# One order for an attention turn, base products issued ahead of the expert weights, loads and stores spread over more queues

## The chip, the cores and the metric

The kernel runs on one core of one Trainium2 chip. The metric is the device time of one execution in microseconds (us); smaller is better. The time before is the median of three runs.

Five engines work side by side, each through its own queue of instructions in order: PE (matrix products, with PEld its weight loads), DVE (vector work, the only one used here for maxima), ACT (scalar functions and copies), POOL (general vector work) and SP (which only issues DMAs). ACT and POOL can issue DMAs too. Matrix products land in eight PSUM banks of 128 x 512 float32.

## The reference, cut to what matters

The input is 2 sequences of 1024 tokens with 512 features. Three blocks follow one another, each on a layer norm (LN) of its input, added to it:

```
x = x + 0.5 * ffn(layernorm(x))
x = x + attn(layernorm(x))
x = x + 0.5 * ffn(layernorm(x))      # the same weights again

ffn(x):   base = x @ W_base.T + b_base                    # 512 x 512
          w    = the 2 largest of softmax(x @ W_router.T), renormalised, 8 experts
          h    = x @ lora_A[e].T  (rank 16, 8 experts = 128 columns)
          base + 2 * sum_e w[e] * (h[e] @ lora_B[e].T)
attn(x):  q, k, v = x @ sign(W).T * scale, cleaned of NaN and infinities
          32 query heads, 8 key/value heads, head size 16
          softmax(q k.T / 4) v, then the output projection of the same kind
```

## The kernel before, in words

**Groups.** Tokens are worked on in groups of 512 (`GT`), written (batch, group): (0,0), (0,1), (1,0), (1,1). A group is four tiles of 128 tokens. `first` does the first FFN, the second LN and q, k, v of a group; `second`, `rest`, `last` and `final` do the output projection and the last FFN. q, k and the attention's output go through DRAM (`qd`, `kd`, `ad`) to be laid out by head.

**An FFN (`ffn_tiles`, line 346).** LN and transposes give `xT`. The router and the rank-16 products come as one matmul of 136 columns (`low`, tile `ph`). Then a chain of small DVE steps picks two experts (lines 385 to 419), the weighted hidden values are transposed and copied to `hT` (line 432), and only then the strands `base(t)` (line 436) are started. Each first adds the bias to the residual on POOL (line 439), does four accumulating matmuls with `wb` (line 444, each two float32 passes), a fifth with `lb` on `hT` (line 448), and adds the result to the residual (line 451 on DVE in the head and the tail, lines 456 and 459 on ACT and POOL during the attention). In the traces, the tiles of the first FFN have names that end in `f`, those of the last FFN names that end in `s`; `hT` is needed by line 448 alone.

**A planner writes the order out.** Each piece of work is a Python generator ("strand") that yields the engine that it needs next: `P` (PE), `v` (DVE), `a` (ACT), `g` (POOL), `d` (SP). `Flow.offer(kind)` gives one step to the first strand by rank whose due time has come; due times and costs are in planner ticks of 0.115 us (`usec`). All of it happens when the program is built: what comes out is a fixed order for each engine. `flow.free` is true in the head (before the attention) and in the tail (after it). `flow.stock` counts what may be held at once, `fb` being PSUM banks: 6 in the head and the tail, 2 for strands during the attention. The pool of banks has 7 and the attention's sums have the eighth.

**The attention (line 868).** There are 32 units (batch, half of the queries, key/value head), each of 4 query heads. A unit takes four turns. A turn does, for three units at different stages: 8 `m` tiles (scores with queries on the partitions, line 785, for the row maxima on DVE, line 793); 8 `e` tiles (transposed scores in two accumulating matmuls, `e0` line 820 and `e1` line 824, the second of which subtracts the maximum, then the exponential on ACT, line 827); and 32 small products with v, `A0` to `A3`, 8 passes each (line 857). An `m` or `e` matmul uses half of the PE's rows, the upper or the lower by the parity of its index, so that two neighbours of different parity run side by side. `A` and the strands' matmuls use all rows. Each `m` and each `e` tile takes a PSUM bank until DVE or ACT has read it.

The order within a turn is written out by hand. Letters are places at which a strand may get a step: `F` for PE, `V` and `W` for DVE, `C` and `D` for ACT; POOL and SP are offered a step after every item. `S` places the maxima of a unit. There are two orders. `FULL` has two `F` (one at either end) and a planned length of 64 ticks, and is taken where PE work of a strand waits; `BARE` has none and 50 ticks:

```
order = (LEAD_IN if not e and not a else FULL if flow.wants("P", begin + at_F)
         else BARE)
span = BRIEF if order is BARE else TICK
```

`need` holds the turns back where q, k or v of a unit are not yet there, and hands out strands' steps until they are.

**The head.** SP issues in this order: the four tiles of x(0,0), `arw` (expert and router weights), `wb` (1 MB), x(0,1), `lb`, then the attention's weights (line 87) with x(1,0) between them. POOL issues the bias `bh` and the scales, then does memsets, among them `two_r` and `mqs` (lines 112 to 117). DVE scales `bh` by one half (line 105). `begin` (line 745) does half of the first unit's `m` tiles when k and the first q of (0,0) are stored, and loads the second half of its keys (`place_k`, line 742) when k of (0,1) is stored. `qkv_part` (line 524) makes each q, k and v item: a scaled copy `y`, cleaning into `o`, then the high part in `y` by ACT (line 568) and the rest in `o` by POOL or DVE (line 571); SP stores both with two DMAs each (line 577).

Of the kernel before, what the change touches and what calls it, by code (L numbers as in the profile page):

```python
# [8 lines left out]
F32 = mybir.dt.float32  # L9
# [6 lines left out]
P = 128  # L16
# [16 lines left out]
def macaron_kernel(ctx: ExitStack, tc: tile.TileContext, x_in, wbT, b_base, wrT, aT, bT,  # L33
# [25 lines left out]
    def load_x(b, g):  # L59
        t = xpool.tile([P, TG, D], F32, tag="x", name=f"x{b}_{g}")  # L60
        for i in range(TG):
            nc.sync.dma_start(t[:, i, :], x_in[b, g * GT + i * P:g * GT + (i + 1) * P, :])
        xg[b, g] = t
# [6 lines left out]
    nc.sync.dma_start(wb, wbT.rearrange("(c p) n -> p c n", p=P))  # L70
# [34 lines left out]
    nc.vector.tensor_scalar(bh, bh, 0.5, None, ALU.mult)  # L105
# [6 lines left out]
    nc.gpsimd.memset(two_r.bitcast(F32), 0.0)  # L112
    for h in range(REP):
        nc.gpsimd.memset(two_r.bitcast(F32)[32 * h:32 * h + 2, h % 2, :], 1.0)
    mqs = [const.tile([P, 512], F32R, name=f"mq{i}") for i in range(3)]
    for t in mqs:
        nc.gpsimd.memset(t.bitcast(F32), 0.0)
# [6 lines left out]
    TICK, BRIEF = 64, 50  # L124
# [15 lines left out]
    class Flow:  # L140
# [79 lines left out]

        def wants(self, kind, by):
            self.settle()
            return any(s.kind == kind and s.at <= by and (kind != "P" or self.lock in (None, s))
                       for s in self.strands)
# [121 lines left out]
    def ffn_tiles(xt, name, rank, tiles, xT, hT, mv, given, mv2, summed, store, loads):  # L346
# [35 lines left out]
        yield "j", list(s2.values())  # L382

# [50 lines left out]
        ready = flow.t  # L434

        def base(t):
            yield "r", dict(t=1)
            yield "g", ""
            nc.gpsimd.tensor_tensor(xt[:, t, :], xt[:, t, :], bh, ALU.add)  # L439
            for c in range(KC):  # L440
                yield ("P", "P") if c else ("P", "", flow.t, 1)
                if c == 0:
                    pb = bank(f"pb{n}_{t}")
                nc.tensor.matmul(pb, xT[:, c, t * P:(t + 1) * P], wb[:, c, :],  # L444
                                 start=(c == 0), stop=False)
                flow.lock = bs[t] if c < KC - 1 else None
            yield "P", "a", ready
            nc.tensor.matmul(pb, hT[0][:, t * P:(t + 1) * P], lb, start=False, stop=True)  # L448
            if flow.free:
                yield "v", "P"  # L450
                nc.vector.scalar_tensor_tensor(xt[:, t, :], pb, 0.5, xt[:, t, :], ALU.mult, ALU.add)
                flow.give(t=1, fb=1)
            else:
                yield "a", "P"
                hb = t512(f"hb{n}_{t}")
                nc.scalar.activation(hb, pb, AF.Copy, scale=0.5)  # L456
                flow.give(fb=1)
                yield "g", "a"
                nc.gpsimd.tensor_tensor(xt[:, t, :], xt[:, t, :], hb, ALU.add)  # L459
                flow.give(t=1)  # L460
            if store is not None:
                yield ("a" if flow.free else "d"), "v" if flow.free else "g"
                (nc.scalar if flow.free else nc.sync).dma_start(store[t * P:(t + 1) * P, :],
                                                                xt[:, t, :])
            if mv2 is not None:
                yield "v", "v" if flow.free else "g"
                stats(xt, t, mv2, n)
                summed.add(t)

        bs = {}  # L470
        for t in tiles:
            bs[t] = flow.spawn(base(t), rank)
# [51 lines left out]
    def qkv_part(b, g, xs, i, fast, at):  # L524
# [40 lines left out]
        if i <= KC:  # L565
            yield "a", "v"
            hi = y[:, :].bitcast(F32R)
            nc.scalar.copy(hi, o)  # L568
# [146 lines left out]
    def places(order, span):  # L715
        w = [LOAD.get(o[0], 0) for o in order]
        return [span * sum(w[:i]) // sum(w) for i in range(len(w))]
# [352 lines left out]
```

## Time and profile before

| | us |
|---|---|
| median of 3 runs | 1160.85 (1159.07 to 1164.19) |
| the profiled execution | 1162.21 |
| its span, first to last instruction | 1160.2 |
| PE, DVE, ACT, POOL busy in the span | 1068.2, 878.5, 669.8, 287.6 |
| mean granted PE clock | 0.968 of full |

The head lasts from 0 to about 162 us (the first products with v start there), the attention to about 1089 us, the tail to the end. "Busy" counts an engine's instructions, and PE's are pipelined: a busy PE is not a PE at its peak. In the windows view each engine's busy time in a stretch is followed by its number of instructions, and the last three columns are the granted PE clock, the busy share of the 16 DMA engines and GB/s.

### The profile page before, as it was taken

The numbers are of one execution on the slowest core, as the hardware profiler recorded it, in microseconds if no ns is written. First come the engines' busy times: TensorE is split into PE (matmuls) and PEld (weight loads), VectorE is DVE, ScalarE is ACT, GpSimd is POOL, SyncE is SP. The second block draws the span as 40 slices with busy tenths as digits, with TensorE's granted clock in tenths as the row PEclk, the third lists the DMA queues.
The fourth block names the chain that finished last, engine by engine and source line by source line (L and its number), as shares of the span: only waits on it lengthen the run. The fifth ranks groups of instructions, "written<-read, shape, count | busy, mean of one in ns | idle before, by whom it ended". The sixth has DMA issues, their size and how long they took to land.

```text
span 1160.2 us, 21527 instructions
## 1 busy us (share of the span) xinstructions
PE 1068.2 (92%) x8453; PEld 589.0 (51%) x8453; DVE 878.5 (76%) x1694; ACT 669.8 (58%) x1309; POOL 287.6 (25%) x337
## 2 busy tenths in 40 slices
PE   3989679999999999999989899999999999999988
PEld 2446435554455554455555455644445555444544
DVE  5577978787788787778788898698779878874372
ACT  2222238765667566667746568665667766666611
POOL 4142632000110031112163322032011213421161
PEclk9989759999999999999989999999999999999989
DMA  8012453121111123214334342112222411221101
GB/s 272 3 61 77 140 174 105 47 47 47 47 47 47 47 83 118 48 40 106 106 87 144 83 114 57 47 47 56 56 65 64 120 45 36 67 84 47 55 24 50
DMA packets 48686, 87.43 MB, mean 75 GB/s; under 512 B 8760, under 2 KB 11832, under 8 KB 48584
## 3 DMA queue, kind: packets, MB, share of 16 engines
q1 hardware_dynamic: 47176, 83.36, 24.9%
q10 hardware_dynamic: 1152, 2.10, 0.5%
q8 instruction: 66, 1.08, 0.4%
q0 software_dynamic: 256, 0.59, 0.3%
q14 instruction: 36, 0.29, 0.1%
HBM read 51.19 MB, written 34.32 MB: 74 GB/s over the span
## 4 chain that ended last, share of the span: by engine, by line
PE 71%; DVE 18%; DMA 3%; ACT 3%; POOL 2%; issue 2%; SPq 0%; POOLq 0%; DVEq 0%; ACTq 0%
PE av L857 19%; PE m L785 15%; DVE mn L793 9%; PE e L820 9%; PE e L824 7%; PE pbf L444 5%; PE pbs L444 4%; PE po L668 2%; ACT es L827 2%; DMA x<-in_x 2%; PE pq L538 2%; PE pv L555 1%; PE pbf L448 1%; PE pbs L448 1%; PE phs L368 1%
## 5 line engine op out<-in xcount | busy, mean ns | idle before, releaser
L793 DVE TENSOR_REDUCE mn<-m 128x1 f32<-128x512 f32 x1024 | 647.6, 681 | 161.5 <-PE e L824 86.0
L827 ACT ACTIVATE es<-e 128x512 f32<-128x512 f32 x1024 | 542.4, 602 | 305.9 <-PE e L824 254.0
L785 PE MATMUL m<-k 64*128 64x512 f32 x1024 | 365.1, 443 | 27.6 <-DMA k<-kd 12.9
L857 PE MATMUL av<-es,vaug 128*32 128x256 f32 x4096 | 277.7, 389 | 18.9 <-ACT es L827 9.3
L820 PE MATMUL e<-k 64*128 64x512 f32 x1024 | 277.8, 443 | 2.7 <-DVE mn L793 2.5
L785 PEld LDWEIGHTS m<-k 64*128 64x128 f32 x1024 | 169.4, 188 | 175.9 <-DVE mn L793 77.8
L824 PE MATMUL e<-mq,two_r 64*128 64x512 f32 x1024 | 255.7, 399 | 1.9 <-DMA mq<-mT 1.9
L857 PEld LDWEIGHTS av<-es,vaug 128*32 128x32 f32 x4096 | 108.6, 110 | 148.8 <-issue 83.9
L820 PEld LDWEIGHTS e<-k 64*128 64x128 f32 x1024 | 121.8, 187 | 61.2 <-DVE mn L793 33.0
L824 PEld LDWEIGHTS e<-mq,two_r 64*128 64x128 f32 x1024 | 144.3, 187 | 14.4 <-issue 2.4
L444 PE MATMUL pbf<-wb,xTf 128*128 128x512 f32 x128 | 64.7, 636 | 0.0
L444 PE MATMUL pbs<-wb,xTs 128*128 128x512 f32 x128 | 61.4, 607 | 0.0
L459 POOL TENSOR_TENSOR x<-x,hbf 128x512 f32<-128x512 f32 x8 | 10.2, 1280 | 161.8 <-ACT hbf L456 161.8
L439 POOL TENSOR_TENSOR x<-x,bh 128x512 f32<-128x512 f32 x32 | 41.4, 1318 | 3.3 <-ACT xns L311 3.1
L444 PEld LDWEIGHTS pbf<-wb,xTf 128*128 128x128 f32 x128 | 24.4, 202 | 28.9 <-issue 27.8
L444 PEld LDWEIGHTS pbs<-wb,xTs 128*128 128x128 f32 x128 | 23.1, 192 | 27.4 <-issue 25.8
L270 POOL TENSOR_TENSOR ro<-ro,loo 128x512 f32<-128x512 f32 x16 | 20.7, 1294 | 58.2 <-DVE ro L268 51.5
L571 POOL TENSOR_TENSOR z<-z,y 128x512 fp32r<-128x512 f32 x17 | 22.7, 1337 | 49.9 <-ACT y L568 49.8
L568 ACT CAST y<-z 128x512 fp32r<-128x512 f32 x20 | 12.5, 626 | 36.5 <-DVE z L274 34.0
L265 POOL TENSOR_SCALAR loa<-y 128x512 f32<-128x512 f32 x17 | 11.7, 687 | 85.0 <-ACT y L543 84.2
L459 POOL TENSOR_TENSOR x<-x,hbs 128x512 f32<-128x512 f32 x8 | 10.3, 1285 | 88.5 <-ACT hbs L456 88.5
L620 POOL TENSOR_TENSOR an<-an,rb 128x512 f32<-128x512 f32 x15 | 19.7, 1316 | 49.8 <-DMA rb<-rd 49.7
(204 smaller groups left out, 1014.6 us busy)
## 6 DMA issues: line engine op xcount, KB each, us to landing
k<-qd SPq DMA_DIRECT2D x32, 512.0 KB
k<-kd SPq DMA_DIRECT2D x62, 256.0 KB
qd<-y SPq DMA_DIRECT2D x32, 256.0 KB
qd<-z SPq DMA_DIRECT2D x32, 256.0 KB
ad<-avs SPq DMA_DIRECT2D x32, 256.0 KB
x<-in_x SPq DMA_DIRECT2D x16, 256.0 KB
an<-ad SPq DMA_DIRECT2D x15, 256.0 KB
rb<-rd SPq DMA_DIRECT2D x15, 256.0 KB
```

Of the source, the lines that this page charges most:

```text
L439: nc.gpsimd.tensor_tensor(xt[:, t, :], xt[:, t, :], bh, ALU.add)
L444: nc.tensor.matmul(pb, xT[:, c, t * P:(t + 1) * P], wb[:, c, :], start=(c == 0), stop=False)
L448: nc.tensor.matmul(pb, hT[0][:, t * P:(t + 1) * P], lb, start=False, stop=True)
L538: nc.tensor.matmul(pq, w_[:, k, :], xs[j][:, k, :], start=(k + j == 0), stop=(k + j == KC))
L571: (nc.vector if fast else nc.gpsimd).tensor_tensor(lo, o, y, ALU.subtract)
L668: nc.tensor.matmul(po, hs[j][:, c, t * P:(t + 1) * P], wo[:, c, :], start=(c + j == 0), stop=(c + j == KC))
L785: nc.tensor.matmul(s["m", i], s["q"][rows_of(h), h // 2, qt * P:(qt + 1) * P], s["k"][rows_of(h), kh * 512:(kh + 1) * 512], start=True, st ...
L793: nc.vector.tensor_reduce(s["mn"][:, 2 * (h % 2) + h // 2, qt, kh:kh + 1], s.pop(("m", i)), AX.X, ALU.max, negate=True)
L820: nc.tensor.matmul(t, s["k"][rows_of(h), kt * P:(kt + 1) * P], s["q"][rows_of(h), h // 2, :], start=True, stop=False)
L824: nc.tensor.matmul(t, two_r[rows_of(h), h // 2, :], s["mq"][rows_of(h), :], start=False, stop=True)
L827: nc.scalar.activation(e, s.pop(("e", i)), AF.Exp, scale=HD ** -0.5)
L857: nc.tensor.matmul(s["av"][32 * h:32 * h + 32, cols], s["v"][:, kt, :], s["es"][kt * REP + h][:, cols], start=(kt + half == 0), stop=(kt + ...
```

## The change

1. **One turn order.** `FULL`, `BARE`, `TICK`, `wants` and `places` go. Every turn but the lead-in uses `TURN`, with 16 `m` and `e` matmuls ahead of `A0`, 8 between `A1` and `A2`, and an `F` at either end. A turn's planned length is 48 ticks and 8 more for each `F` that gave a step.
2. **Base ahead of the router's result.** In the head and the tail (`early`), the strands `base(t)` start as soon as the 136-column matmuls are done, and wait for `hT` only before the fifth matmul. During the attention they start where they did.
3. **Loads.** The last two tiles of x(0,0) and `wb` are issued by ACT instead of SP.
4. **Stores by makers.** For the items of batch 0 that are not marked fast (three of (0,0), four of (0,1)), ACT issues the two stores of `y` right after line 568, and POOL the two of `o` after line 571.
5. **Constants.** The halving of `bh`, and POOL's memsets of `two_r` and `mqs`, become a strand of low rank that starts 12 to 14 us into the plan. `begin` and `base` wait for them in the plan.
6. The sign matrix of the output projection gets rank 8 instead of 5.5, and the planner's arrival times for x(0,0) are 3, 3.7, 6.6 and 7.3 us instead of 4, 5, 6, 7.

```diff
     def load_x(b, g):
...
-            nc.sync.dma_start(t[:, i, :], x_in[b, g * GT + i * P:g * GT + (i + 1) * P, :])
+            eng = nc.scalar if b == g == 0 and i >= 2 else nc.sync
+            eng.dma_start(t[:, i, :], x_in[b, g * GT + i * P:g * GT + (i + 1) * P, :])
...
-    nc.sync.dma_start(wb, wbT.rearrange("(c p) n -> p c n", p=P))
+    nc.scalar.dma_start(wb, wbT.rearrange("(c p) n -> p c n", p=P))
...
-    nc.vector.tensor_scalar(bh, bh, 0.5, None, ALU.mult)
...
-    TICK, BRIEF = 64, 50
+    BRIEF, SLICE = 48, 8
...
         yield "j", list(s2.values())
+        def base(t):
+            if not early:
+                yield "r", dict(t=1)
+            yield "u", lambda: "bias" in signs
+            yield "g", ""
+            nc.gpsimd.tensor_tensor(xt[:, t, :], xt[:, t, :], bh, ALU.add)
+            for c in range(KC):
+                yield ("P", "P") if c else ("P", "", flow.t, 1)
...
+            yield "u", lambda: ready
+            yield "P", "a", ready[0]
+            nc.tensor.matmul(pb, hT[0][:, t * P:(t + 1) * P], lb, start=False, stop=True)
...
+        bs, ready, early = {}, [], flow.free
+        if early:
+            for t in tiles:
+                bs[t] = flow.spawn(base(t), rank)
...
-        ready = flow.t
...
+        ready.append(flow.t)
+        if not early:
+            for t in tiles:
+                bs[t] = flow.spawn(base(t), rank)
...
+            own = b == 0 and i < KC and not fast
             yield "a", "v"
             hi = y[:, :].bitcast(F32R)
             nc.scalar.copy(hi, o)
+            if own:
+                for c in range(2):
+                    nc.scalar.dma_start(dst[:, 2 * c, :, :], y)
             yield "v" if fast else "g", "a"
             lo = o[:, :].bitcast(F32R)
             (nc.vector if fast else nc.gpsimd).tensor_tensor(lo, o, y, ALU.subtract)
-            for j, t in enumerate((y, o)):
+            if own:
+                for c in range(2):
+                    yield "g", "", None, 5
+                    nc.gpsimd.dma_start(dst[:, 2 * c + 1, :, :], o)
+            for j, t in enumerate(() if own else (y, o)):
...
-    FULL = ("V F W m0(3) e0(4) e0(7) e0(2) m0(7) e1(4) e1(7) e1(2) A0 A1 S C e0(6) e0(3) e1(6) "
-            "e0(1) m0(4) V e1(1) m0(0) e1(3) A2 A3 m0(1) e0(0) C e0(5) m0(6) e1(5) e1(0) m0(5) D "
-            "m0(2) F")
-    BARE = ("A0 A1 e0(2) C m0(7) e1(2) e0(3) e0(4) e0(1) m0(0) e1(3) e1(1) C e1(4) m0(1) m0(6) S A2 "
-            "A3 m0(3) e0(0) V e0(5) D e1(0) e0(7) e0(6) e1(5) m0(2) e1(7) V e1(6) W m0(5) m0(4)")
+    TURN = ("F e0(7) m0(6) e1(7) e0(2) e1(2) m0(1) D V e0(5) e0(4) e1(5) e1(4) e0(6) e0(3) e1(6) "
+            "e1(3) m0(5) m0(0) S A0 C V A1 m0(2) e0(1) e0(0) C m0(3) e1(0) e1(1) W m0(4) m0(7) A2 "
+            "A3 F")
...
-        yield "u", lambda: {(0, 0, KC), (0, 0, 0)} <= ended
+        yield "u", lambda: {(0, 0, KC), (0, 0, 0)} <= ended and "maxima" in signs
...
-            order = (LEAD_IN if not e and not a else FULL if flow.wants("P", begin + at_F)
-                     else BARE)
-            span = BRIEF if order is BARE else TICK
-            at = places(order, span)
+            order = LEAD_IN if not e and not a else TURN
+            done = given = 0
...
-                flow.t = max(flow.t, begin + at[pos])
+                flow.t = max(flow.t, begin + BRIEF * done // loads[id(order)] + SLICE * given)
+                done += LOAD.get(kind, 0)
...
-                    flow.offer("P")
+                    given += flow.offer("P")
...
+            span = BRIEF + SLICE * given
...
-        yield from binarize(wraw["o"], D, "o", osc, 5.5, usec(36))
+        yield from binarize(wraw["o"], D, "o", osc, 8, usec(36))
...
-        flow.spawn(first(0, 0, ..., [usec(4 + t) for t in range(TG)]), 0)
+        flow.spawn(later_constants(), 7)
+        flow.spawn(first(0, 0, ..., [usec(t) for t in (3, 3.7, 6.6, 7.3)]), 0)
```

## The prediction

> **What bounds the kernel now.** First the page: who is busy, and in which slice of 29 us.
>
> ```profile
> PE 1068.2 (92%) x8453; PEld 589.0 (51%) x8453; DVE 878.5 (76%) x1694; ACT 669.8 (58%) x1309; POOL 287.6 (25%) x337
> ...
> PE   3989679999999999999989899999999999999988
> ...
> DVE  5577978787788787778788898698779878874372
> ...
> PEclk9989759999999999999989999999999999999989
> ```
>
> PE sets the attention; the head (the first five and a half slices) is ragged, and its clock drops in slices 4 and 5. The windows view sizes that.
>
> ```profile
> 0.00:28.00 28.00, 9.22 (x52) 8.54 (x52) 15.33 (x57) 6.16 (x15) 13.81 (x28) 0.92 0.87 279
> 28.00:100.00 72.00, 64.20 (x219) 34.64 (x219) 49.81 (x116) 19.00 (x47) 19.83 (x22) 0.91 0.13 43
> 100.00:148.00 48.00, 34.96 (x158) 24.23 (x158) 43.77 (x76) 12.14 (x22) 26.74 (x25) 0.82 0.41 115
> 148.00:162.00 14.00, 8.74 (x25) 4.47 (x25) 10.06 (x21) 3.79 (x7) 7.98 (x10) 0.56 0.40 121
> 1089.00:1160.20 71.20, 59.81 (x250) 35.00 (x248) 35.36 (x106) 16.09 (x37) 24.63 (x25) 0.95 0.11 41
> ```
>
> In the head PE is busy 117.1 us of 162 and DVE 119.0. PE is full from 28 to 100 while DVE idles 22.2; from 100 to 148 DVE is full (91%). They take turns at waiting for each other. The timeline and the waits at line 451 tell why.
>
> ```profile
> 8.16 0.43 DVE L105 TENSOR_SCALAR bh<-bh 128x512 f32<-128x512 f32 x1 [3.98 <-DMA bh<-in_b_base]
> 31.25 4.84 PE L444 MATMUL pbf<-wb,xTf 128*128 128x512 f32 x8
> 132.63 2.04 PE L785 MATMUL m<-k 64*128 64x512 f32 x6 [9.75 <-DMA k<-kd]
>   PE pbf L448: 15.2, 7
> ```
>
> DVE stands 3.98 us behind the bias's DMA with x already there. The base products start at 31.25, after `hT` (its copy starts at 29.70), although the router's matmuls ended at 19.9 and PE did little in between. DVE then waits 15.2 us in 7 waits for `pbf`, the first FFN's base sums.
>
> Two attention turns in PE's timeline, one of each order:
>
> ```profile
> 837.30 0.49 PE L785 MATMUL m<-k 64*128 64x512 f32 x1
> ...
> 838.43 1.13 PE L448 MATMUL pbs<-lb,hTs 128*128 128x512 f32 x2
> ...
> 840.35 0.49 PE L785 MATMUL m<-k 64*128 64x512 f32 x1
> ...
> 841.46 1.07 PE L857 MATMUL av<-es,vaug 128*32 128x256 f32 x16
> 842.46 0.50 PE L820 MATMUL e<-k 64*128 64x512 f32 x2
> ...
> 843.59 1.07 PE L857 MATMUL av<-es,vaug 128*32 128x256 f32 x16
> 844.59 0.50 PE L785 MATMUL m<-k 64*128 64x512 f32 x1
> ```
>
> Start to start: 8 `m`/`e` matmuls take 1.12, 16 `A` passes 1.00, the two `F` steps (four passes) 1.92. FULL = 3 x 1.12 + 2 x 1.00 + 1.92 = 7.28 (837.30 to 844.59). A BARE turn beside it (892.01 to 897.46) has blocks of 12 at 1.70 and 1.75: 5.45. Over the trace I count 90 FULL turns (mean 7.47) and 36 BARE (mean 6.46 without the two longest). From 176 to 1074 us blocks of 8 average 1.23, blocks of 12 average 2.10: FULL is near its floor, BARE is held up by DVE (8 maxima at about 0.60 apart are 4.8 us, and strands' steps come on top).
>
> **The change part by part.**
>
> *Bias and constants.* The halving leaves the front of DVE's queue: -3.98. POOL's memsets (4.78 to 7.48) leave the way of the first `rstd`; their later run lies in POOL's idle time.
>
> *Base early, head.* For each group 4 x 3.43 = 13.7 us of base passes move from behind `hT` into PE's idle time before it; behind `hT` stay 4 x 0.86 us of `lb`. Of the gain the path sees what DVE waited for: 15.2. The cover: `wb` must have landed. It lies ahead of x(0,1), whose first tile lands at 18.19, so `wb` comes by about 17, and PE, in order, could stand up to 2 us before it; nothing behind it is ready earlier. Four base sums hold four of the six banks until `hT`; group (0,1) may wait for one, which the ranks make the lesser evil. POOL's bias adds move ahead of the expert choice. Today they run beside it (23.40 to 28.37), where line 414 takes 1.12 instead of 0.17: perhaps 3 us more, not counted.
>
> Next late is DVE, full from 100 us. So the head gains 3.98 + 15.2 = 19. Bounds: 5, if DVE's work after 100 swallows all but the start; 39, if DVE's whole idle time but the first 3.5 us goes (162 - 119 - 3.5).
>
> *Loads.* DMA is 87% busy at 279 GB/s until 28 us, so a second queue saves issue time only: 1.82 us for four x tiles on SP becomes 0.9 each on two. x tiles wait for bytes. I take 0 (0 to -1).
>
> *Stores.* 28 DMAs leave SP: 14 go to ACT (0.6 us each by the SP rows, 8.4 us, where ACT is busy 12 of 48), 14 to POOL (0.56 to 0.79 by its first five, 8 to 11 us, where POOL has 21 of 48 idle). Queued behind them are exponentials on ACT and cleaning steps on POOL; both have that idle time as cover, without it +11. SP no longer stands behind a `y` that isn't made (a store at 127.49 sits just before the key load at 128.18). But that load also followed the last maximum of `begin` (126.72 + 0.67), so its 9.75 us stall of PE shrinks by little: 0 (-5 to +3).
>
> The Trainium skill, "SBUF — State Buffer", Who interferes with whom, speaks against POOL's stores: POOL writes their descriptors through a port that DVE's two-port operations lock, so such a DMA waits while DVE works. POOL's five loads here took 6.3 to 11.2 us to land, with DVE mostly idle, so their slowness has another cause. By the rule these q items land later still; the sum stays, since the third unit's load, the first to read such an item, is issued at 167.28, 47 us after that item's cast (119.86).
>
> *Turn order.* PE's items stay 24 + 32 + fills. TURN has blocks of 16 and 8; with fills A, F, then 16 is one change of shape fewer than FULL. A block of 16 is at least 1.12 + 4 pairs x 0.23 = 2.04 and, counted as two blocks, 2.24. Without fill: 2.04 + 1.12 + 2.00 = 5.16 to 5.36 (BARE 5.45); with: 7.08 to 7.28 (FULL 7.28).
>
> Against it: banks. The first block asks for 10 new ones within 1.7 us; FULL never asks for more than 6 between pauses, BARE for 8. From the rows a maximum starts about 0.5 us after its matmul and they follow at 0.60, exponentials at 0.48. The first four banks come back at about 1.2, 1.4, 1.8 and 1.9. With one of the seven held by a base sum, the last pair (due at 1.72) needs four: +0.2. With two held it needs five: +0.6. Then a filled turn is 0.2 better to 0.4 worse than FULL. One base sum is held most of the time, two only while ACT copies the older out: I take +0.1, 90 x 0.1 = +9. BARE turns are set by DVE: -0.1 x 36 = -4.
>
> One turn, at 577.3, takes 20.92 us: `need` waits for batch 1's q, k, v and pours 9.2 us of their matmuls in. 5.45 + 9.24 = 14.7 is work, 6.2 is waiting and a cold clock. Places in every turn bring that chain forward: -5. Attention: 9 - 4 - 5 = 0, from 90 x -0.2 - 36 x 0.29 - 6 = -34 to 90 x 0.4 = +36.
>
> *Tail.* PE ends at 1155.8 and is busy 59.8 of those 66.8: 7.0 idle, part of it before `hT` of the last two half groups. -4 (0 to -7).
>
> **Sum.** Against the profiled execution (1162.21, which is 1.4 above the median): 1162.2 - 19 + 0 - 4 = 1139; against the median 1138.
>
> **The rivals.**
>
> *Banks decide (slower).* Two banks held through most filled turns: +36, head and tail still -23: 1174. It turns from gain to loss at 23/90 = 0.26 us a filled turn. For: ten banks in 1.7 us against a supply of four. Against: one base sum at a time, locked, and the 1.92 us pause at the turn's start lets DVE and ACT catch up.
>
> *TURN is dense.* Turns at 7.1 and 5.2, chains earlier: -34 - 23: 1104. Against: BARE's mean of 6.46 is DVE's work, which no order removes.
>
> *Head swallowed.* DVE's 91% from 100 to 148 eats the 15.2; only the bias's 4 and the tail's 4 stay, turns as forecast: 1153. For: 43.8 us of DVE work there is the same after. Against: the work of that stage can start earlier.
>
> **How the numbers follow.** Forecast with its terms partly met (1118 to 1155): 0.52. Dense: 0.15. Head swallowed: 0.15, half of it below 1155. Banks: 0.18. Half a per cent, about what this measurement can tell, is 1155.0 to 1166.7. Faster: 0.52 + 0.15 + 0.05 = 0.72, since "swallowed" with some bank stalls is the same; same 0.11; slower 0.17. The range for 8 in 10 leaves out the far parts of both outer rivals: 1112 to 1168; the forecast's own is 1118 to 1155.
>
> **What would show it.** Right: no bias wait on DVE before 5 us; `pbf` from about 16 us with its `lb` passes apart; DVE's wait for `pbf` under 4; first `A` at about 143; turns with base fill at 7.2 to 7.4. Wrong: blocks of 16 over 2.5 us in filled turns, PE waiting for `mn` or `es` there; the first `A` after 157; a key load landing later because of POOL's stores.

## The result and the profile after

The changed kernel takes 1167.41 us (median of 19 runs, 1164.69 to 1172.31), the kernel before 1162.33 beside it (19 runs): a ratio of 1.0058 [1.0044, 1.0071], so it is slower by 0.6%. The profiled execution took 1167.24 us with a span of 1165.5, 5.3 us more than before's span of 1160.2. Three stretches of PE's timeline make up the difference, cut at the start of the first `av` matmul ("first A") and the end of the last:

| | first A | first A to last A | last A to the end |
|---|---|---|---|
| before | 164.8 | 927.7 | 67.7 |
| after | 162.2 (-2.6) | 939.3 (+11.6) | 64.0 (-3.7) |
| forecast | -19 | 0 | -4 |

The page's busy times and slices, after:

```profile
PE 1089.9 (94%) x8453; PEld 604.2 (52%) x8453; DVE 868.1 (74%) x1694; ACT 660.9 (57%) x1309; POOL 295.7 (25%) x351
...
PE   6879579999999999999999999999999999999978
...
DVE  6678987766787766787878987886677766797462
PEclk9999679999999999999999999999999999999999
```

PE does more in the first slice (6, it was 3), but slice 5 dips to 5 (it was 6). Its busy time rises by 21.7 us for the same 8453 matmuls, so what the change cost sits among instructions that the page counts as busy, not in idle time. The windows view, in the stretches shown of before and for the last 71.2 us:

```profile
0.00:28.00 28.00, 17.25 (x70) 12.63 (x71) 16.89 (x72) 6.75 (x17) 15.06 (x28) 1.00 0.90 284
28.00:100.00 72.00, 61.70 (x248) 37.48 (x247) 51.27 (x112) 21.31 (x51) 19.96 (x23) 0.95 0.15 46
100.00:148.00 48.00, 34.10 (x124) 20.48 (x123) 46.05 (x73) 10.23 (x16) 34.21 (x38) 0.78 0.47 128
148.00:162.00 14.00, 8.66 (x39) 5.64 (x39) 11.69 (x21) 7.96 (x16) 6.33 (x7) 0.64 0.77 202
1094.30:1165.50 71.20, 58.63 (x256) 32.70 (x248) 34.01 (x81) 14.35 (x32) 27.10 (x27) 0.95 0.13 45
```

By 28 us PE has done 8 us more than before. From 100 to 148 DVE is busy 46.05 of 48 us (before 43.77). From 148 to 162 the DMAs carry 202 GB/s instead of 121. In the last stretch PE is busy 1.2 us less than before. The instructions of the head that were shown of before, the wait for `pbf`, and a new wait:

```profile
10.54 0.42 DVE L998 TENSOR_SCALAR bh<-bh 128x512 f32<-128x512 f32 x1
14.43 5.72 PE L358 MATMUL phf<-arw,xTf 128*128 128x136 f32 x32 [1.67 <-DMA arw<-in_wrT]
19.99 3.60 PE L383 MATMUL pbf<-wb,xTf 128*128 128x512 f32 x8
  DVE x L391: 7.1, 3
153.75 0.76 PE L824 MATMUL e<-mq,two_r 64*128 64x512 f32 x1 [4.90 <-DMA mq<-mT]
```

The bias no longer holds DVE up, the base products start at 19.99 instead of 31.25 (forecast: about 16), DVE's wait for them is 7.1 us instead of 15.2 (forecast: under 4), and the 9.75 us wait for the second key half is gone. Much of what was forecast of the first 100 us is there, yet the first A is only 2.6 us earlier.

A turn with a fill, in PE's timeline:

```profile
829.65 1.98 PE L383 MATMUL pbs<-wb,xTs 128*128 128x512 f32 x4
831.56 0.50 PE L820 MATMUL e<-k 64*128 64x512 f32 x1
...
833.90 1.07 PE L857 MATMUL av<-es,vaug 128*32 128x256 f32 x16
834.90 0.50 PE L785 MATMUL m<-k 64*128 64x512 f32 x1
...
836.33 1.07 PE L857 MATMUL av<-es,vaug 128*32 128x256 f32 x16
837.33 1.13 PE L383 MATMUL pbs<-wb,xTs 128*128 128x512 f32 x2
```

`F` 1.91, the block of 16 2.34, `A` 1.00, the block of 8 1.43, `A` 1.00: 7.68, where FULL's turn took 7.28. In the block of 16 the second pair comes 0.34 us behind the first, the next three at 0.23 to 0.24, and from there on the steps are 0.26 to 0.42. Who waits, in the list of waits (total us, times, longest):

```profile
ACT es L827 <- PE e L824: 332.7, 215, 4.8
DVE mn L793 <- PE m L785: 182.6, 168, 3.9
```

Before, these were 254.0 and 32.5. But an `m` and an `e` run side by side, and a wait may stand under the name of either. The page's rows for the maxima, before and then after, have the whole idle time of DVE before them (behind the second bar), and what ended it:

```profile
L793 DVE TENSOR_REDUCE mn<-m 128x1 f32<-128x512 f32 x1024 | 647.6, 681 | 161.5 <-PE e L824 86.0
...
L793 DVE TENSOR_REDUCE mn<-m 128x1 f32<-128x512 f32 x1024 | 646.0, 681 | 206.9 <-PE m L785 182.6
```

So DVE is idle 45 us longer before the maxima, and ACT 30 us longer before the exponentials (336.1 instead of 305.9). PE's weight loads for `m` and `e` wait 150 us in all for a maximum or an exponential to end, where they waited 156: not more, but elsewhere, in every turn instead of in single long ones ("Places in every turn", below).

### The profile page after: what moved, and what is told of

It reads as the page before. It is cut to its first block, busy times and chain, and to the rows that moved or that the text cites. A ratio compares the mean times of both kernels' runs of the same rounds, so it can differ in the third digit from the quotient of the medians.

```text
span 1165.5 us, 21569 instructions
## 1 busy us (share of the span) xinstructions
PE 1089.9 (94%) x8453; PEld 604.2 (52%) x8453; DVE 868.1 (74%) x1694; ACT 660.9 (57%) x1309; POOL 295.7 (25%) x351
## 4 chain that ended last, share of the span: by engine, by line
PE 73%; DVE 16%; DMA 4%; issue 3%; ACT 2%; POOL 1%; SPq 1%; POOLq 0%; DVEq 0%; ACTq 0%
PE av L857 18%; PE e L820 13%; PE m L785 12%; DVE mn L793 9%; PE e L824 8%; PE pbf L383 5%; PE pbs L383 4%; PE po L674 2%; PE pq L536 2%; PE phs L358 1%; DMA mq<-mT 1%; PE pbf L388 1%; PE pv L553 1%; PE phf L358 1%; ACT es L827 1%
## 5 line engine op out<-in xcount | busy, mean ns | idle before, releaser
L793 DVE TENSOR_REDUCE mn<-m 128x1 f32<-128x512 f32 x1024 | 646.0, 681 | 206.9 <-PE m L785 182.6
L827 ACT ACTIVATE es<-e 128x512 f32<-128x512 f32 x1024 | 537.1, 615 | 336.1 <-PE e L824 332.7
L785 PE MATMUL m<-k 64*128 64x512 f32 x1024 | 352.5, 449 | 13.1 <-DVE mn L793 5.6
L820 PE MATMUL e<-k 64*128 64x512 f32 x1024 | 332.9, 449 | 3.6 <-ACT es L827 0.9
L857 PE MATMUL av<-es,vaug 128*32 128x256 f32 x4096 | 276.1, 387 | 12.6 <-issue 11.2
L824 PE MATMUL e<-mq,two_r 64*128 64x512 f32 x1024 | 273.5, 402 | 7.9 <-DMA mq<-mT 7.8
L785 PEld LDWEIGHTS m<-k 64*128 64x128 f32 x1024 | 155.7, 187 | 129.7 <-ACT es L827 68.4
L820 PEld LDWEIGHTS e<-k 64*128 64x128 f32 x1024 | 148.7, 185 | 118.2 <-DVE mn L793 50.6
L824 PEld LDWEIGHTS e<-mq,two_r 64*128 64x128 f32 x1024 | 139.2, 187 | 17.8 <-issue 9.3
L383 PE MATMUL pbf<-wb,xTf 128*128 128x512 f32 x128 | 61.0, 605 | 0.0
L630 POOL TENSOR_TENSOR anxL<-an,anxT 128x512 fp32r<-128x512 f32 x15 | 19.1, 1284 | 54.4 <-ACT anxT L628 50.4
L687 POOL TENSOR_TENSOR yo<-yo,osc 128x512 f32<-128x512 f32 x12 | 17.3, 1441 | 60.0 <-ACT yo L682 32.2
```

Source lines behind the costliest of these rows:

```text
L785: nc.tensor.matmul(s["m", i], s["q"][rows_of(h), h // 2, qt * P:(qt + 1) * P], s["k"][rows_of(h), kh * 512:(kh + 1) * 512], start=True, st ...
L793: nc.vector.tensor_reduce(s["mn"][:, 2 * (h % 2) + h // 2, qt, kh:kh + 1], s.pop(("m", i)), AX.X, ALU.max, negate=True)
L820: nc.tensor.matmul(t, s["k"][rows_of(h), kt * P:(kt + 1) * P], s["q"][rows_of(h), h // 2, :], start=True, stop=False)
L824: nc.tensor.matmul(t, two_r[rows_of(h), h // 2, :], s["mq"][rows_of(h), :], start=False, stop=True)
L827: nc.scalar.activation(e, s.pop(("e", i)), AF.Exp, scale=HD ** -0.5)
L857: nc.tensor.matmul(s["av"][32 * h:32 * h + 32, cols], s["v"][:, kt, :], s["es"][kt * REP + h][:, cols], start=(kt + half == 0), stop=(kt + ...
```

## The experiments

In the table, "net" is a turn (from one first `A` to the next) less the PE time of its fills, median and mean, counted from the trace over the 127 turns; a block's mean is counted from about 176 us to near the last A. Each row is one execution: open_half and open_final (below), which differ behind the attention alone, are 2.5 us apart in the first A and 3.8 in the attention, so smaller differences between two rows tell nothing.

| kernel | first A | first to last A | rest | blocks of m and e, mean us | net, turns with fill | net, without |
|---|---|---|---|---|---|---|
| before | 164.8 | 927.7 | 67.7 | 8: 1.23, 12: 2.10 | 5.57, 5.86 | 5.59, 6.12 |
| after | 162.2 | 939.3 | 64.0 | 16: 2.67, 8: 1.34 | 5.98, 5.98 | 6.15, 6.13 |
| turn_only | 164.9 | 938.3 | 65.8 | 16: 2.71, 8: 1.32 | 5.97, 6.00 | 6.04, 6.04 |
| head_only | 157.1 | 926.9 | 74.0 | 8: 1.25, 12: 2.09 | 5.57, 5.90 | 5.58, 5.97 |
| one_fill_bank | 162.8 | 937.1 | 66.4 | 16: 2.62, 8: 1.39 | 5.88, 5.97 | 6.00, 6.16 |
| six_banks | 164.8 | 1007.2 | 63.6 | 16: 3.19, 8: 1.42 | 6.63, 6.66 | 6.42, 6.31 |
| twelves | 162.5 | 925.7 | 68.4 | 12: 1.99 | 5.81, 5.95 | 6.01, 6.06 |
| full_open | 163.0 | 903.7 | 71.6 | 8: 1.20; 28 of 16: 3.10 | 5.58, 5.66 | 6.21, 6.22 |
| spread_half | 160.1 | 984.1 | 65.0 | 8: 1.32 | 5.79, 6.03 | 6.40, 6.70 |

The theory after the result: in the attention a bunch of 16 runs out of banks, and in the head DVE's full stretch from 100 us on swallows what the base products gain. The rivals: an offer of a fill in every turn makes turns long, or the head leaves the attention in another state; and the new stores, or a chain through other engines and DMAs, hold the head.

### The two halves apart: turn_only, head_only

turn_only is the kernel before with the new `TURN` and its planning; head_only is the changed kernel with the old ones.

```diff
-    FULL = (...)   BARE = (...)   TICK, BRIEF = 64, 50
+    TURN = (...)                  BRIEF, SLICE = 48, 8
```

> The kernel before with nothing but the new turn order and its planning (TURN, SLICE, an F that may stay empty); head, loads, stores and base order as before. Theory (the block of 16 is short of banks): the first av matmul stays at about 164.8 us and the stretch from the last av matmul to the end at about 67.7; the attention takes 939 instead of 928, blocks of 16 average 2.6 to 2.7, and the run is about 11 us slower than before (1.010). Rival A (the attention's loss is made by the changed head, whose chains arrive in another state): attention 928, ratio 1.000. Rival B (TURN is dense, as one of the prediction's rivals had it): attention 900 or less, ratio 0.97.

> The changed kernel with FULL, BARE and their planning put back in the attention; early base, late constants, loads over two queues and stores by makers stay. Theory: first av matmul at 162 (2.6 earlier than before), attention 928, end stretch 64: about 6 us faster than before (0.995). The prediction's own sum without its turn term: 23 us faster (0.980). Rival A (the head spoils the attention): attention 939, ratio 1.004.

turn_only: 1.0094 [1.0069, 1.0118], attention 938.3 as expected. Rival A and rival B fall: the loss belongs to the turn order. head_only: 0.9990 [0.9976, 1.0004]. Its head gains 7.7 where 2.6 was expected, and its attention is as before, but the rest is 74.0, 6.3 more, which no theory had: so it misses the expected 0.995.

### What in TURN costs: full_open, twelves, one_fill_bank, six_banks, spread_half

full_open has FULL's order as the only one, so that with a fill no block is longer than 8:

```diff
-    TURN = ("F e0(7) m0(6) ...16... S A0 C V A1 ...8... A2 A3 F")
+    TURN = ("V F W ...8... A0 A1 S C ...8... A2 A3 ...8... D m0(2) F")
```

> The changed kernel whose one turn order is FULL's (blocks of 8, 8 and 8 round the A pairs, F between the last and the first), with places that may stay empty as in TURN. With a fill in F no block is longer than 8. Theory (block of 16 short of banks): filled turns fall from about 7.9 to 7.5 us, attention about 915 (the shorter stretch at the batch's change, 13 us, is kept), total about 24 us below the changed kernel: ratio to before 0.985. Rival C (an offer in every turn makes turns long, not the block): attention 935 to 940 as now, ratio 1.005.

0.9848 [0.9827, 0.9870], 1142.71 us: the expected number. Attention 903.7, the block of 8 at 1.20. A turn of it and its waits:

```profile
799.37 1.07 PE L855 MATMUL av<-es,vaug 128*32 128x256 f32 x16
...
801.50 1.07 PE L855 MATMUL av<-es,vaug 128*32 128x256 f32 x16
...
803.64 1.98 PE L383 MATMUL pbs<-wb,xTs 128*128 128x512 f32 x4
...
806.68 1.07 PE L855 MATMUL av<-es,vaug 128*32 128x256 f32 x16
```

```profile
L791 DVE TENSOR_REDUCE mn<-m 128x1 f32<-128x512 f32 x1024 | 645.2, 681 | 152.8 <-PE e L822 88.5
```

Taking 1.00 for each `A` and 1.92 for `F`, the blocks take 1.13, 1.14 and 1.12: 7.31 in all. DVE is idle 152.8 us before maxima, where it was 206.9. Rival C (an offer in every turn makes turns long) falls: 96 turns have a fill, about as many as after's 94, and they are as short as FULL's before. Of the 24 us that the attention gains on before, 8 are fills that now run behind it (165 us of them in the attention instead of 173), which the longer rest shows.

twelves uses BARE's two blocks of 12 with an `F` at either end:

```diff
+    TURN = ("F ...12... S A0 V A1 ...12... A2 A3 F")
```

> The changed kernel with BARE's two blocks of 12 as its one order, F ahead of the first and behind the second, S, V, C and the like in the places of TURN. Theory (what costs is how many banks a block asks for without a pause: 6 in blocks of 8, 8 in blocks of 12, 10 in TURN's 16): blocks of 12 at 1.8 to 2.0, against a floor of 1.70, attention between the 904 of FULL's order and the 939 of TURN: 910 to 925. Rival D (what costs in TURN is the kind of steps in its block, not its length): attention within 5 us of 904 or of 939.

0.9963 [0.9945, 0.9982]; blocks at 1.99, attention 925.7, at the edge of the 910 to 925 expected. Against floors of 1.12 and 1.70 (the shortest in the traces) and 2.24 (twice 1.12) the mean blocks of 8, 12 and 16 are 0.08, 0.29 and 0.43 over.

The banks themselves: one_fill_bank takes one from the chains' share, six_banks takes one from the pool.

```diff
-        flow.stock["fb"] -= 4
+        flow.stock["fb"] -= 5                                  # one_fill_bank
-    ps = ctx.enter_context(tc.tile_pool(name="ps", bufs=7, ...
+    ps = ctx.enter_context(tc.tile_pool(name="ps", bufs=6, ...   # six_banks, fb=5, fb -= 3
```

> The changed kernel with one bank instead of two that chains may hold at a time in the attention, so that at least six of seven are left for m and e. Theory: the blocks of 16 fall from a mean of 2.67 to 2.4 or less and those of 8 from 1.34 to 1.25; turns with fills gain up to 0.36 each, but fewer fills are ready when F is reached, so the chains take more turns and the need waits may grow: attention 910 to 945. Rival C (not the banks): blocks of 16 stay at 2.6 to 2.7 and the attention is as long or longer (939 to 960).

> The changed kernel with six rotating PSUM banks instead of seven; the chains may still hold two in the attention (five instead of six in the head), so m and e lose the one. Theory (the block of 16 stalls because its ten new banks exceed what is free): blocks of 16 grow from a mean of 2.67 to 2.9 to 3.2, blocks of 8 by less than half of that, attention 25 us or more longer. Rival (the stall is the pace of DVE and ACT, whatever the banks): blocks of 16 within 0.1 of 2.67.

one_fill_bank: 1.0064 [1.0039, 1.0090], blocks of 16 at 2.62. The theory's number fails. six_banks: 1.0688 [1.0656, 1.0719]; the 16 grow by 0.52 to 3.19, the 8 by 0.08. That is the expected pattern, and the pace of DVE and ACT, unchanged, cannot make it. DVE's idle time before maxima (206.9) becomes 272.4, ACT's before exponentials (336.1) 403.9.

The traces also show where a block stops. In `TURN` the sixth new bank of a block of 16 is asked for by its eighth matmul, the seventh by its eleventh. Counted over the 119 blocks, matmuls that start within 0.06 us of the end of a maximum or an exponential, which gives a bank back:

| | sixth bank | seventh bank |
|---|---|---|
| after | 31 | 105 |
| one_fill_bank | 9 | 101 |
| six_banks | 113 | 104 |

The ninth, tenth, thirteenth and fourteenth matmul, which take no new bank, do so in 1 block at most. So as a rule one of after's seven banks is held elsewhere and the block stops at its seventh; a second is held in about a quarter of the blocks, which fits the little that taking it from the fills gained.

spread_half tries to rid full_open of the blocks of 16 that are left in its 31 turns without a fill (8 and 8 join there):

```diff
-    "... A0 A1 ...8... A2 A3 ...8... F"
+    "... A0 ...8... A1 A2 ...8... A3 F"       # and the stores of half_stores, below
```

> As open_half, with the A passes spread: one A behind the first block of 8, two behind the second, one ahead of F, so that a turn without a fill has no block of 16 either (with FULL's order 8 and 8 join there, at a mean of 3.10 us). Theory (pauses between blocks let banks come back): the joined blocks vanish, each of the some 30 turns without a fill gains up to 0.6 us, filled turns stay at 7.3: 10 to 18 us faster than open_half. Rival (a pause of 0.5 is too short for the banks of a block of 8, so blocks of 8 grow from 1.20 to 1.35 and more): no gain, or some us slower.

1.0427 [1.0404, 1.0450], a miss, with the rival's sign: blocks of 8 grow from 1.20 to 1.32, and the `A` passes of a turn take 0.57 + 1.05 + 0.57 instead of twice 1.00. Against open_half (attention 910.0), which has the same stores, the mean net turn grows from 5.69 to 6.03 with a fill and from 6.24 to 6.70 without (93 x 0.34 + 34 x 0.46 = 47 us), and 26 us more of fills fall into the attention (195 instead of 169), 73 of the 74 us together. That fits a pause of 0.57 being too short for the banks of a block of 8.

### The head: early_alone, no_early, sp_stores, half_stores

```diff
+        bs, ready, early = {}, [], flow.free      # early_alone: into the kernel before, with base(t)
-        bs, ready, early = {}, [], flow.free
+        bs, ready, early = {}, [], False          # no_early: in the changed kernel
-            own = b == 0 and i < KC and not fast
+            own = False                           # sp_stores
+            own = b == g == 0 and i < KC and not fast   # half_stores
```

> The changed kernel with base products behind hT everywhere, in the head too; loads over two queues, late constants and stores by makers stay. The forecast (15.2 us of the head by the early base): first av matmul at 175 or later. Theory (head swallowed: what the base products gain before 100 us is eaten by DVE's full stretch from 100 us on): DVE waits 13 to 15 us for pbf again, its busy time from 28 to 100 falls by some us, and the first av matmul comes at 163 to 167, no more than 5 us later.

> The kernel before with nothing changed but the base products: they start beside the router's matmuls where the bank allows, in the head and in the last stretch; bias, loads, stores, constants and turn orders as before. The forecast's term (15.2 us of DVE's waits for pbf go): first av matmul at about 150. Theory 1 (early base worth 13, the other head changes cost 10): 150 to 153. Theory 2 (head swallowed from 100 us on by DVE's queue): last base sum of the second group 6 to 10 us earlier than 93.6, but the first av matmul at 158 to 164.

no_early: 1.0177 [1.0156, 1.0198], first A 175.4, 13.2 later: the forecast's 15.2 looked right, and the theory's 163 to 167 failed. early_alone: 1.0033 [1.0020, 1.0046], first A 163.1, 1.7 earlier: theory 2's number, swallowed. So the parts don't add. In no_early the chain of waits (start, us, what) shows what the other head changes cost without the early base: the load of x(1,1) (line 63) waits on SP for the output weights' signs, is issued ahead of the second unit's q, which then takes 8.15 us to land.

```profile
134.25 0.35 SPq L63
...
136.06 8.15 DMA k<-qd
```

In early_alone the last base sum of (0,1) is early too (81.72, before 93.61), but PE then waits 9.48 us for the second key half, whose load stands on SP behind stores: the 17th `m` comes at 131.2, before at 132.6. DVE is not full there, as theory 2 had it: from the end of the last base sum to the first `e1` it is busy 56 of 70 us.

> The changed kernel with the stores of the first batch's q items back on SP, all four of an item behind its cleaning. Theory (DVE, full from 100 us on, sets the head; POOL's 14 descriptors and ACT's 14 stand in the way of the cleaning steps): POOL's busy time from 100 to 148 falls from 34.2 to about 27, the first av matmul comes at 158 to 161 instead of 162.2, and the run is 1 to 4 us faster than the changed kernel. Rival (SP stands behind an item that isn't made, as the change's stores by makers avoid): the second key half lands late again, PE waits for it near the 17th m tile as before (up to 9.75 us), first av matmul at 163 to 168.

> The changed kernel with stores by makers for the first group's q items alone; those of the second group go back to SP, where they stand behind the mq copy. Theory (the second group's stores from ACT and POOL, in flight at 144 to 154, slow the mq copy): PE's wait for mq falls from 4.90 to about 1.95 us, the second key half still lands without a 9 us stall, first av matmul at 158 to 160. Rival (DVE's queue holds the head as it is): first av matmul at 161 to 163 although the copy is faster. Attention as in the changed kernel, 938 to 942.

sp_stores: 1.0053 [1.0035, 1.0071], no different from after; first A 163.4. half_stores: 1.0048 [1.0029, 1.0067]; first A 160.9, between what the theory and the rival had. In sp_stores PE waits 9.44 us for the second key half again (at 130.23). In half_stores the wait for `mq` is that of before:

```profile
151.56 0.76 PE L824 MATMUL e<-mq,two_r 64*128 64x512 f32 x1 [1.95 <-DMA mq<-mT]
```

Stores by makers take away 9.4 us of waiting for keys, and the first A comes 1.2 earlier, which two single rows can't tell from nothing; the 256 KB stores of the second group, in flight at 148 to 154, cost 2.95 at the `mq` copy. In half_stores SP issues a store 0.7 us behind that copy, and PE still goes on 1.9 us after the copy's issue; with the stores on ACT's and POOL's queues it takes 4.8. In head_only, which has stores by makers too, none is issued from 140 to 150, and PE's wait for `mq` is 1.96. The Trainium skill ("DMA: Bandwidth & Descriptors", Queues, rings and completion order) says that a DMA engine takes turns between the queues that have work for it, a packet at a time; these two runs agree: a store on the copy's own queue stands behind it, one on another queue shares the engines with it.

### Who holds the stretch from 100 us on: q_uncleaned, x11_late, light_head, open_light

The chain of waits of after, in part:

```profile
122.57 2.45 DVE rs_o L493 x3
...
128.90 0.61 DVE stf L269
...
142.65 1.15 DVE osc L508
```

From 103.6 to 148 nearly every piece is DVE's, those that the first A doesn't need (`rs_o`, `osc`, `stf`) among them.

```diff
+        if b == 0 and i < KC and not fast: nc.scalar.copy(o_, y_)   # q_uncleaned, in place of finite()
+        yield "u", lambda: ("mq", 1) in ended     # x11_late, ahead of load_x(1, 1)
+        yield "u", lambda: ("mq", 0) in ended     # light_head, ahead of binarize(wraw["o"]...)
-        chains = [(0, lambda g=g: first(1, g, ...
+        chains = [(LEAD + 1, lambda g=g: first(1, g, ...      # light_head
```

> The changed kernel without the cleaning of non-finite values for the first batch's q items that are not fast (six or seven of eight; ACT copies the item instead): three DVE operations and two POOL operations fewer for each, about 2.8 us of DVE each, some 15 us of them between 100 us and the first av matmul. Theory (DVE's work sets the time from 100 us to the first av matmul): first av matmul 10 to 16 us earlier, at 146 to 152. Rival (a chain of waits through PE, ACT, POOL and the DMAs sets it, DVE is only busy beside it): first av matmul within 4 us of 162.2.

> The changed kernel with one move: the load of x(1,1) (1 MB on SP, issued at 149.8, just behind the copy of the first unit's maxima to mq) waits until the second unit's mq copy is issued. Theory (that load shares the DMA engines with the 8 KB copy that PE waits for): the copy lands 1.9 us after its issue instead of 4.8, PE's wait of 4.90 falls to about 1.95, first av matmul at 159 instead of 162.2, run 3 us faster than the changed kernel. Rival (PE would have stood there for DVE's maxima anyway): first av matmul at 162 again.

> The changed kernel with work that the first av matmul doesn't need moved behind it: the weights of the output projection are made after the first mq copy, and the second batch's chains start six turns later. No work is left out. Theory (from 103 us on the path is DVE's queue: in the chain of waits nearly all pieces from 103.6 to 148 are DVE's, with 5.1 us for w_o and about 3.2 us of statistics for x(1,0) among them, then 4.7 us of the mq copy): first av matmul 8 to 11 us earlier, at 151 to 154; if the attention's turns swallow the moved work in places that would have stayed empty, the run is 6 to 10 us faster than the changed kernel. Rival (another chain of about the same length stands behind DVE's, as without the cleaning of the q items): first av matmul at 158 to 162.

q_uncleaned (1.0612 [1.0582, 1.0643]): first A 162.0, the rival's number. Its chain:

```profile
132.33 11.52 DMA x<-in_x
143.87 0.70 DVE stf L269
```

DVE, in order, stands behind the statistics of x(1,1), whose load took 11.5 us among the stores (205 GB/s from 100 to 148): the freed DVE time went into a DMA wait at once. Its whole time says nothing more, since 159 us of chains are left behind the last A. x11_late (1.0177 [1.0160, 1.0194]): PE's wait for `mq` stays 4.91, so x(1,1) is not what slows that copy (half_stores then showed what does), and the later load cost 11 us in the attention. light_head (1.0257 [1.0238, 1.0275]): the second unit's first `m` comes at 130.1 instead of 141.3, 11.2 earlier, so the work moved away did hold that stretch. It is DVE's, ACT's and POOL's, and no run moves DVE's part alone. But with the stores now bunched closer to it the `mq` copy lands later:

```profile
148.72 0.76 PE L825 MATMUL e<-mq,two_r 64*128 64x512 f32 x1 [9.22 <-DMA mq<-mT]
```

Of the 11.2 us 5.0 are left at this first `e1` and 3.8 at the first A, where 8 to 11 were expected. The chains that started later cost 28 us in the attention: one unit, at the batch's change, takes 55.3 from its first `A` to the next unit's, instead of 31.1. open_light adds FULL's order as in full_open to light_head:

> Both lessons: FULL's order with places that may stay empty, and the head without the work that the first av matmul doesn't need. If the two gains add: first av matmul at 152 to 155, attention 904 as with FULL's order alone, the rest 64 to 72: about 1128 to 1133 us, ratio to before 0.972 to 0.976. If the chains that start later pile up at the end, the last stretch is longer than 75 and the gain of the head is lost: ratio 0.985.

1.0025 [1.0012, 1.0037], 22 worse than full_open alone: that unit takes 72.8. The pile-up was expected at the end; it came at the batch's change.

### The end, and the versions that follow: early_head_only, open_half, open_final

```diff
+        bs, ready, early = {}, [], flow.free and not flow.after   # early_head_only, open_final
```

> The changed kernel in which the base products are early in the head alone; in the last stretch, after the attention, they come behind hT as before. Head and attention unchanged (162.2; 939). The forecast's tail term (early base gains 4 us there): the stretch behind the last av matmul goes from 64.0 to 68. Theory now (the end's length comes mostly from how much chain work the attention left over; the kernel with the new turn order alone had 65.8): 65 to 66. Rival (four base sums ahead of the second half group's router hold PE, so early is worse there): 60 to 62.

> FULL's order with places that may stay empty and the stores of half_stores. Theory: attention about 904, head as in half_stores: 1138 to 1142 us, ratio to before 0.980 to 0.984; if the stores make no difference to the head, 0.985.

> FULL's order with places that may stay empty, the second group's stores on SP, and the early base in the head alone. Theory (in the last stretch the early base products of one half group stand ahead of the other's router on PE, the engine that is full there): the stretch behind the last av matmul falls from 71.4 to 65 to 67, and the run to 1136 to 1139 us, ratio to before 0.978 to 0.981. Rival (the stretch's length is what the attention left over, 26 us of chains, not the early base): 70 to 72 and 0.985.

early_head_only: 1.0062 [1.0041, 1.0083], rest 64.7 against after's 64.0. open_half, full_open with half_stores: 0.9856 [0.9831, 0.9881], rest 71.4 (its head is 6.4 earlier than full_open's, 156.6, and its attention 6.3 longer, so the 0.980 to 0.984 expected did not come); open_final, open_half without the early base at the end: 0.9858 [0.9834, 0.9882], rest 73.4, where 65 to 67 was expected. So the early base gains 0.7 to 2.0 there with these orders, too little to be told from nothing. In early_alone, with the old ones, the rest is 73.8 against 67.7: it loses 6.1 (the transposes ahead of the last `hT` start 64.3 us behind the last A instead of 45.5), and head_only shows the same (74.0 and 64.7). Why the sign differs stays open. full_open, open_half and open_final are equally fast, and faster than both kernels: about 1143 us.

## Why the prediction was wrong

**Bias: -3.98 forecast, about 0.** The wait is gone, but the router's matmuls then waited for `arw` until 14.43 and ended at 20.15, before at 19.93. The sum let DVE's start count without asking what the step behind it waited for.

**Early base: -15.2 forecast.** Locally it came: the last base sum of (0,0) is added at 37.80 instead of 49.86, that of (0,1) at 83.60 instead of 93.61. Then it shrinks: the second unit's first `m` is 7.3 earlier, the first A 2.6. The failed step is "of the gain the path sees what DVE waited for": behind the last base sum lies a stretch in which DVE is nearly full, and that stretch grew. The windows view, from the end of the last base sum to the first `e1`, before and then after:

```profile
94.30:154.38 60.08, 43.59 (x192) 28.51 (x190) 55.69 (x100) 15.59 (x29) 32.48 (x32) 0.82 0.33 92
84.30:153.75 69.45, 47.95 (x198) 29.93 (x197) 64.01 (x105) 17.15 (x33) 41.62 (x49) 0.81 0.43 116
```

It is 9.4 us longer, and DVE is busy 8.3 us longer in it, with 5 instructions more. What the prediction set against the rival "head swallowed", "the work of that stage can start earlier", so holds for few steps. Most of the rest is that the steps on q, k and v items (`z`, `ma`, `vd`) take longer: 28 of 0.67 us in the mean before, 31 of 0.83 after. Line 258 takes 0.41 us where no POOL operation overlaps it and 1.51 to 2.09 where one does for 1.2 to 1.3 us; and with the stores back on SP (sp_stores), POOL less busy by 7 us, the 31 steps take 0.70. The `mq` copy adds 2.95. No run shows how much of the gain each of these took, and it stays open why head_only, with the same head changes and the old turn orders, has its first A 7.7 earlier instead of 2.6. The rival "head swallowed", at 0.15, came true in its sum: of its 8, 6.3 were found in head and end together, but the head's 2.6 are not the bias's 4.

**Loads and stores: 0 forecast, about 0 found**, but as the balance of a 9.4 us wait removed against +2.95 at the `mq` copy and these longer steps on DVE. Of the rule of the Trainium skill ("SBUF — State Buffer", Who interferes with whom) that spoke against POOL's stores, no run shows a sign: the fourteen landed in a median of 8.7 us, no later than POOL's five loads before.

**The turn: +0.1 forecast, +0.41 found.** The banks' price in the rival "banks decide", 0.4 a filled turn, was met in the median, by luck: it stood for two banks held, and mostly one was. The mis-sized term is the forecast's +0.1. It had the first four banks back 1.2, 1.4, 1.8 and 1.9 us into the block; in the 87 blocks behind an `F` the matmuls that wait for the seventh to the tenth bank start at 1.48, 1.56, 2.07 and 2.18 in the mean. Turns without a fill were to gain 0.1 and lost 0.56 (5.59 to 6.15): there a block of 16 follows an `A` and takes 2.95 in the mean, behind an `F` 2.57. By the medians that is 94 x 0.41 + 33 x 0.56 = 57 us.

**Places in every turn: -5 forecast, about -45 found.** Before, the mean turn lies 0.29 (with fill) and 0.53 (without) above its median, 97 x 0.29 + 30 x 0.53 = 44 us of single long turns; after, it lies at it. The unit with the turn that began at 577.3 takes 31.1 instead of 44.3. The same sum is 44 and 45 in head_only and early_alone, which have the old orders, and 4 in turn_only: so the long turns go with the two orders and their planning. Offers in every turn and planned lengths changed together, and no run parts them. This is the gain of the change, and 57 - 45 = 12 is what the attention lost: its forecast of 0 missed by little because two large misses nearly cancel. Blocks of 8 with the same offers keep most of the gain (8 us of long turns are left) without the price: full_open.

**End: -4 forecast, -3.7 found, for another reason in part:** the turn order alone gives 1.9 of it, the early base 0.7 (early_head_only), and 1.1 belongs to neither alone; each is too small to be told from nothing in single rows.

Of the signs named ahead, three for "wrong" came: blocks of 16 over 2.5 us, PE waiting for `mn` and `es` there, and a first A after 157. The fourth, a key load landing later because of POOL's stores, did not: PE's wait for the second key half went away. Of the 28 us between the forecast's -23 and the +5.3 found, 16 are the head's and 12 the attention's.

## What to carry to other kernels

An order for matmuls that each take a bank is sized by how many banks it asks for between two pauses, not by how few changes of shape it has: here, of 7 banks, 6 cost 0.1 us a block, 8 cost 0.3 and 10 cost 0.4. A wait that is removed ahead of a stretch in which an engine is nearly full need not shorten the whole: here 10 us became 2.6, since steps and small copies in that stretch paid for the work and the traffic that the change moved beside them. Where turns are of two kinds, compare medians and means apart: a change can make every turn worse and the sum about the same.

## What was not expected of the hardware

PE went on 1.9 us after the issue of an 8 KB copy from SBUF to SBUF in before and half_stores, 4.8 (after) to 9.1 (light_head) with 256 KB stores in flight. With 8 `A` passes between `m` and `e` matmuls the pause takes 0.57 us, with 16 1.00: the 8 passes more take 0.43, so a change there and back costs about 0.14, an estimate from these two pauses (0.57 - 0.43).
